# A two-layer graph network: used columns of the adjacency matrix listed on the chip and gathered by indirect DMA

## Chip, cores, metric

One core of a Trainium2 chip (trn2). Times are device microseconds (us) of one execution; each figure is the median of the fast runs of one kernel. Engines: PE is TensorE (PEld its weight loads), DVE VectorE, ACT ScalarE, POOL GpSimd, SP SyncE. "Row tile" means 128 of the 2708 nodes; there are 22, the last with 20 rows.

## The reference, cut

```python
def _gat_head(h, node_adj, edge_adj, W, a):
    hW = h @ W
    hp = (node_adj > 0).astype(hW.dtype) @ hW
    hm = (node_adj < 0).astype(hW.dtype) @ hW
    e_plus = leaky_relu(concatenate([hp, hm], axis=1) @ a, ALPHA)[:, 0]
    # ... e_minus for negative entries
    att = where(edge_adj > 0, e_plus[None, :], NEG_INF)
    att = softmax(where(edge_adj < 0, e_minus[None, :], att), axis=1)
    return att * edge_adj @ hW

# layer 0; adj0 is adj without its diagonal d
h = relu(layernorm(x))
edge = gru(adj0 @ h, h, edge weights)
node = gru(mean over 3 heads of _gat_head(h, adj0, adj0, W_i, a_i), h, node weights)
x = x + d * edge + d * node
# layer 1: the softmax over neighbours has one logit per row, so it is a mean over neighbours
h = relu(layernorm(x))
x = x + layernorm(mean over j with adj[i, j] > 0 of (h @ W)_j) * gamma + beta
```

`x` is 2708 x 256 and `adj` 2708 x 2708 in float32. Of `adj` 10,885 entries off the diagonal are set, 0.15%, all of them positive; the diagonal is at least 0.05.

## The kernel before

It treats `adj` as dense: everywhere 22 chunks of 128 columns for each row tile. The three parts that the change replaces:

```python
# 1. slabs of adj^T (512 columns): node support and logits
for n0, nn in slabs:
    for m0, g in mgroups:
        nc.sync.dma_start(at[:mr, :g, :nn], src...)            # adj^T
        nc.vector.tensor_scalar(pm, at, 0.0, None, op0=ALU.is_gt)
        # ... mm with is_lt, mask written to DRAM for layer 1
        for j in range(g):
            for c in range(KC):
                nc.tensor.matmul(pns[:, c, :nn], lhsT=h_sb[:mr, m, c*P:(c+1)*P], rhs=at[:mr, j, :nn], ...)
            # ... two mask products for the logits
    # ... logits to all partitions (E), edge GRU for each row tile

# 2. attention by rows of adj
for t in range(NT):
    nc.sync.dma_start(A[:r], adj[t*P : t*P + r, :])
    for i in range(HEADS):
        nc.gpsimd.memset(L[:r], NEG_INF)
        nc.vector.copy_predicated(L[:r], pos[:r], E[:r, i, :])
        nc.vector.copy_predicated(L[:r], neg[:r], E[:r, HEADS + i, :])
        nc.vector.tensor_reduce(nmax[:r], L[:r], AX.X, ALU.max, negate=True)
        nc.scalar.activation(L[:r], L[:r], AF.Exp, bias=nmax[:r], accum_out=den[:r])
        nc.gpsimd.tensor_tensor(L[:r], L[:r], A[:r], op=ALU.mult)
        # 22 transposes of L, 22 copies from PSUM, 22 products with h
    # ... head weights, node GRU

# 3. layer 1: 22 x 22 blocks of the mask times h in three bf16 parts
for t in range(NT):
    for m in range(NT):
        for s, (c0, cn) in enumerate(parts):
            nc.tensor.matmul(ps[:r, :cn], lhsT=mask[:, m, t*P : t*P + r], rhs=hs[:, m, c0:c0+cn], ...)
```

## Time and profile before

| | before |
|---|---|
| median of 4 runs | 2337.9 us (2334.8 to 2341.2) |
| PE / DVE / POOL busy | 1999 / 1411 / 632 us |
| layer norm and head vectors | 0 to 84 us |
| slabs, edge GRU | 84 to 640 us (556) |
| dense attention, node GRU | 640 to 2062 us (1422) |
| layer 1: preparation, mask products | 2062 to 2342 us (77 + 203) |

An engine is "busy" while it runs instructions; where PE is near 100% of a stage, as in the slabs, PE bounds it, and where no engine is, as in attention, they take turns. The lines are in the prediction.

### The profile page before, as it was taken

What the parts mean: (1) busy time and instruction counts of PE and PEld (TensorE: products, weight loads), DVE (VectorE), ACT (ScalarE), POOL (GpSimd) and SP (SyncE); (2) the same over time, 40 slices, a digit from 0 to 9 for tenths busy, and PEclk for the clock granted to TensorE, in tenths of its full rate; (3) what the DMA queues carried; (4) which work ended last, traced back from release to release, by engine and by line L of the source; (5) the groups of instructions that cost most, each with busy time, mean ns of one, the idle gap of its engine ahead of it and who ended that gap; (6) DMA issues with size and microseconds to landing.
All of it is one profiled execution on the core that took longest, in us unless ns stands there. A gap on an engine that the chain in (4) does not pass through costs nothing.

```text
span 2341.6 us, 21972 instructions
## 1 busy us (share of the span) xinstructions
PE 1998.8 (85%) x8718; PEld 1298.2 (55%) x8718; DVE 1410.9 (60%) x1655; ACT 568.2 (24%) x1100; POOL 631.6 (27%) x270
## 2 busy tenths in 40 slices
PE   3899999999938888898888888888888898869985
PEld 2333334343526666676666666666666676436774
DVE  5422233322285868878687778686868878355444
ACT  1110101000112333333333333333333333222000
POOL 1000000000034443344333443334443343201323
PEclk9979798987968999998999999999999999978998
DMA  3322130301110000000000000000000000030000
GB/s 102 129 81 68 51 91 31 117 21 33 56 40 24 25 24 24 24 24 24 24 24 24 24 18 17 14 24 24 24 24 24 25 4 1 1 136 6 15 17 14
DMA packets 52591, 86.40 MB, mean 37 GB/s; under 512 B 8536, under 2 KB 32378, under 8 KB 49782
## 3 DMA queue, kind: packets, MB, share of 16 engines
q1 hardware_dynamic: 26782, 70.35, 8.9%
q10 hardware_dynamic: 25708, 14.66, 2.1%
q8 instruction: 68, 1.11, 0.2%
q14 instruction: 33, 0.27, 0.0%
HBM read 74.89 MB, written 10.11 MB: 36 GB/s over the span
## 4 chain that ended last, share of the span: by engine, by line
PE 54%; DVE 24%; issue 9%; POOL 6%; ACT 4%; DMA 2%; ACTq 0%; POOLq 0%; SPq 0%; DVEq 0%
PE pq L355 17%; DVE L L333 11%; PE pns L276 10%; DVE L L334 5%; DVE nmax L336 5%; PE pn L166 4%; PE prz L161 3%; PE prz L159 3%; PE ptr L349 3%; PE pn L167 2%; PE pb L298 2%; ACT wT L353 2%; PE prz L162 2%; POOL L L332 2%; PE pe L284 2%
## 5 line engine op out<-in xcount | busy, mean ns | idle before, releaser
L355 PE MATMUL pq<-h_sb,wT 128*128 128x256 f32 (+2 forms) x2904 | 753.0, 405 | 198.6 <-ACT wT L353 193.8
L355 PEld LDWEIGHTS pq<-h_sb,wT 128*128 128x128 f32 (+2 forms) x2904 | 537.9, 196 | 335.8 <-ACT wT L353 244.3
L341 POOL TENSOR_TENSOR L<-L,A 128x2708 f32<-128x2708 f32 (+1 forms) x66 | 393.3, 5960 | 489.5 <-ACT L L338 489.5
L333 DVE COPY_PREDICATED L<-pos,E 128x2708 f32<-128x2708 uint8 (+1 forms) x66 | 394.3, 5976 | 131.1 <-POOL L L332 130.9
L332 POOL MEMSET L<- 128x2708 f32 (+1 forms) x66 | 155.3, 2354 | 898.2 <-DVE x_sb L182 580.7
L353 ACT COPY wT<-ptr 128x512 f32<-128x512 f32 (+3 forms) x462 | 204.6, 479 | 465.9 <-PE ptr L349 465.6
L349 PE MATMUL ptr<-ident,L 128*128 128x128 f32 (+2 forms) x1452 | 223.6, 287 | 32.2 <-POOL L L341 32.2
L276 PE MATMUL pns<-at,h_sb 128*128 128x512 f32 (+2 forms) x528 | 239.7, 574 | 1.1 <-DVE at L263 1.1
L338 ACT ACTIVATE L<-L,nmax 128x2708 f32<-128x2708 f32 (+1 forms) x66 | 168.6, 2555 | 240.4 <-DVE nmax L336 240.4
L349 PEld LDWEIGHTS ptr<-ident,L 128*128 128x128 f32 (+2 forms) x1452 | 176.2, 146 | 85.3 <-POOL L L341 33.3
L334 DVE COPY_PREDICATED L<-neg,E 128x2708 f32<-128x2708 uint8 (+1 forms) x66 | 218.3, 3310 | 1.8
L336 DVE TENSOR_REDUCE nmax<-L 128x1 f32<-128x2708 f32 (+1 forms) x66 | 196.0, 2971 | 1.5
L440 PE MATMUL ps<-hs,mask 128*128 128x256 bf16 (+4 forms) x1452 | 164.3, 272 | 18.0 <-ACT hp L445 18.0
L440 PEld LDWEIGHTS <-mask 128*128 128x128 fp8e4 (+3 forms) x1452 | 137.7, 96 | 44.5 <-issue 27.0
L175 DVE TENSOR_TENSOR o<-h_sb,n 128x256 f32<-128x256 f32 (+1 forms) x44 | 134.2, 3050 | 14.0 <-ACT n L173 11.1
L276 PEld LDWEIGHTS pns<-at,h_sb 128*128 128x128 f32 (+1 forms) x528 | 87.2, 192 | 99.4 <-issue 95.4
L253 DVE TENSOR_SCALAR pm<-at 128x1536 fp8e4<-128x1536 f32 (+3 forms) x48 | 39.1, 815 | 159.4 <-PE pe L284 152.5
L171 DVE SCALAR_TENSOR_TENSOR n<-rz,pn 128x256 f32<-128x256 f32 (+1 forms) x44 | 18.3, 416 | 189.9 <-PE pn L167 184.8
L113 POOL TENSOR_TENSOR rstd<-v,mhalf 128x1 f32<-128x1 f32 x66 | 36.2, 551 | 304.3 <-DVE v L111 262.0
L340 DVE RECIPROCAL rden<-den 128x1 f32<-128x1 f32 (+1 forms) x66 | 10.8, 163 | 134.6 <-ACT L L338 134.6
L366 PE MATMUL pes<-qT,w 128*128 128x128 f32 (+1 forms) x528 | 84.7, 295 | 0.3 <-ACT qT L133 0.3
L366 PEld LDWEIGHTS pes<-qT,w 128*128 128x128 f32 x528 | 78.1, 214 | 3.0 <-issue 0.4
(133 smaller groups left out, 1730.2 us busy)
## 6 DMA issues: line engine op xcount, KB each, us to landing
A<-in_adj_dram SPq DMA_DIRECT2D x21, 1354.0 KB, 5.7
at<-in_adjT_dram SPq DMA_DIRECT2D x35, 768.0 KB, 4.3
mask<-mask_dram SPq DMA_DIRECT2D x21, 338.5 KB, 6.2
mask_dram<-pm ACTq DMA_DIRECT2D x35, 192.0 KB, 4.6
x_sb<-in_x_dram SPq DMA_DIRECT2D x1, 2688.0 KB, 10.8
out_dram<-y ACTq DMA_DIRECT2D x21, 128.0 KB, 1.7
at<-in_adjT_dram SPq DMA_DIRECT2D x7, 222.0 KB
w<-in_L_gnn_gat_W_dram SPq DMA_DIRECT2D x3, 256.0 KB, 2.8
```

What stands on the lines that cost most here:

```text
L276: nc.tensor.matmul(pns[:, c, :nn], lhsT=h_sb[:mr, m, c * P : (c + 1) * P], rhs=at[:mr, j, :nn], start=first, stop=last,)
L332: nc.gpsimd.memset(L[:r], NEG_INF)
L333: nc.vector.copy_predicated(L[:r], pos[:r], E[:r, i, :])
L334: nc.vector.copy_predicated(L[:r], neg[:r], E[:r, HEADS + i, :])
L336: nc.vector.tensor_reduce(nmax[:r], L[:r], AX.X, ALU.max, negate=True)
L338: nc.scalar.activation(L[:r], L[:r], AF.Exp, bias=nmax[:r], accum_out=den[:r])
L341: nc.gpsimd.tensor_tensor(L[:r], L[:r], A[:r], op=ALU.mult)
L349: nc.tensor.transpose(ptr[:mr, j, :r], L[:r, (m + j) * P : (m + j) * P + mr], ident[:r, :r])
L353: nc.scalar.copy(wT[:mr, :g, :r], ptr[:mr, :g, :r])
L355: nc.tensor.matmul(pq[:r], lhsT=wT[:mr, j, :r], rhs=h_sb[:mr, m + j, :], start=(m + j == 0), stop=(m + j == NT - 1),)
L366: nc.tensor.matmul(pes[:, c, :r], lhsT=w[:, k, i, c * P : (c + 1) * P], rhs=qTs[i][:, k, :r], start=(i == 0 and k == 0), stop=(i == HEADS ...
L440: nc.tensor.matmul(ps[:r, :cn], lhsT=mask[: rows(m), m, t * P : t * P + r], rhs=hs[: rows(m), m, c0 : c0 + cn], start=(m == 0 and s == 0), ...
```

## The change

Its intent: do work only for columns that are used. Columns are cut into five ranges (`NG` = 5). For each row tile and range the kernel lists the used columns, at most 128 of them, with compares and small products; an indirect DMA then gathers these rows of adj^T (`S`), and all products run on 5 gathered chunks instead of 22. The tables that the products need (h with the exponentials of the logits; later h of layer 1 in three bf16 parts) are written to DRAM and gathered with the same lists. Flags (among them more than 128 used columns, negative entries, large logits, a row without any entry) decide whether the old program runs after all. The GRUs now work on slabs of four row tiles. Cut to its core:

```diff
+    bad = compressed_path(tc, *args)
+    with tc.If(bad > 0):
+        general_path(tc, *args)          # the old program

+            for j in range(NT):                                   # lists
+                nc.sync.dma_start(at[:mr], adjT[j*P : j*P + mr, :])
+                nc.vector.tensor_reduce(reach[:mr, j, :NFULL], at..., AX.X, ALU.max, apply_absolute_value=True)
+                nc.vector.tensor_scalar(used[:, j, :], reach[:, j, :], 0.0, None, op0=ALU.is_gt)
+                # place = rank of each used column in its range, by two small products
+                for t in range(NT):
+                    nc.vector.tensor_scalar(onehot[:, t, :], iota1, place[:, j, t:t+1], None, op0=ALU.is_equal)
+                # ... for each range g: 22 products onehot x (tile, row, 1, logit parts) add up lists[g]
+                # when range g is complete:
+                    for t in range(NT):
+                        nc.gpsimd.indirect_dma_start(
+                            S[:, t, g, : rows(t)], None, adjT,
+                            bass.IndirectOffsetOnAxis(ap=idxa[:, g, t:t+1], axis=0), element_offset=t*P)
+                        if edges[g] < t*P + rows(t) and edges[g+1] > t*P:      # own block: drop the diagonal
+                            nc.vector.tensor_scalar_add(own, ia[:, t:t+1], -float(t*P))
+                            nc.vector.scalar_tensor_tensor(blk, iota0, own, blk, op0=ALU.not_equal, op1=ALU.mult)
+            # ... masks, logits, exp, the columns of htab

+            for s in range(...):                                  # main: slabs of 4 row tiles
+                for t in ts:
+                    for g in range(NG):
+                        nc.gpsimd.indirect_dma_start(hg, None, htab, ...idxh[:, g, t:t+1]...)
+                        nc.scalar.copy(sv[:, 0, :r], S[:, t, g, :r])
+                        for i in range(HEADS):
+                            nc.vector.tensor_scalar(sv[:, 1+i, :r], S[:, t, g, :r], hg[:, D+i:D+i+1], None, op0=ALU.mult)
+                        for k in range(KC):
+                            nc.tensor.matmul(pq[k][:, :, :r], lhsT=hg[:, k*P:(k+1)*P], rhs=sv[:, :, :r], ...)
+                    # ... counts, normalizers (dg, pb, rb), nsT and qT
+                ds, ns = gru(edge, nsT, ...); ...; ds, ns = gru(node, esT, ...)
+                    # in gru: nc.gpsimd.tensor_tensor(d, h, n, op=ALU.subtract)
+                    # after it: nc.gpsimd.tensor_tensor(osum, osum, n, op=ALU.add)
+                # ... transposes pt, x of layer 1, its layer norm (rs by POOL's power), rows of h1tab

+        for t in range(NT):                                       # layer 1
+            for g in range(NG):
+                nc.gpsimd.indirect_dma_start(hg, None, h1tab, ...idxh[:, g, t:t+1]...)
+                for s, (c0, cn) in enumerate(parts):
+                    nc.tensor.matmul(ps[:r, :cn], lhsT=mask[:, t, g, :r], rhs=hg[:, c0:c0+cn], ...)
+            # ... mean, product with W, layer norm (rs by POOL's power), out
```

## The prediction

> **What bounds the kernel now.** I read first the shares and the forty slices, then the busy time by stage (I set the stage borders at the first and last instruction of each program part), then the groups and single rows.
>
> ```profile
> PE 1998.8 (85%) x8718; PEld 1298.2 (55%) x8718; DVE 1410.9 (60%) x1655; ACT 568.2 (24%) x1100; POOL 631.6 (27%) x270
> PE   3899999999938888898888888888888898869985
> ...
> DVE  5422233322285868878687778686868878355444
> ```
>
> PE is busiest, but only in slices 3 to 11 does it stand at 9. By stage (columns: length, then busy time and instructions of PE, weight loads, DVE, ACT, POOL; granted clock; DMA share; GB/s):
>
> ```profile
> 84.00:640.00 556.00, 553.17 (x1353) 208.69 (x1352) 164.92 (x303) 52.38 (x102) 0.00 (x0) 0.89 0.23 71
> 640.00:2062.00 1422.00, 1190.14 (x5565) 890.18 (x5564) 1061.22 (x483) 460.95 (x817) 549.19 (x136) 0.92 0.06 21
> ...
> 2139.00:2342.00 203.00, 164.63 (x1455) 137.81 (x1453) 92.90 (x437) 13.18 (x45) 59.75 (x88) 0.96 0.04 15
> ```
>
> The slabs of adj^T (556 us) are bound by TensorE alone. The dense attention (1422 us, 61% of the span) has PE at 84% and DVE at 75%, neither full: PE, DVE and POOL take turns. The mask products of layer 1 (203 us) are PE again. All three multiply by matrices whose entries are nearly all zero. What attention costs:
>
> ```profile
> L355 PE MATMUL pq<-h_sb,wT 128*128 128x256 f32 (+2 forms) x2904 | 753.0, 405 | 198.6 <-ACT wT L353 193.8
> ...
> L341 POOL TENSOR_TENSOR L<-L,A 128x2708 f32<-128x2708 f32 (+1 forms) x66 | 393.3, 5960 | 489.5 <-ACT L L338 489.5
> L333 DVE COPY_PREDICATED L<-pos,E 128x2708 f32<-128x2708 uint8 (+1 forms) x66 | 394.3, 5976 | 131.1 <-POOL L L332 130.9
> ...
> L336 DVE TENSOR_REDUCE nmax<-L 128x1 f32<-128x2708 f32 (+1 forms) x66 | 196.0, 2971 | 1.5
> ```
>
> **What the Trainium skill says.**
> 1. "TensorE: Matmul & The Clock Gate", Back-to-back issue gap: N columns take N/2.4 + 2.5 ns warm. The trace agrees, if a float32 product counts as four passes (two instructions of two): the rows below start 1.71 us apart for two products of 512 columns, 0.855 us each. That stretch has clock 1.00; the slab stage as a whole got 0.89.
>
> ```profile
> 283.30 1.88 PE L159 MATMUL prz<-whh_e,hT 128*128 128x512 f32 x4
> 285.01 1.88 PE L161 MATMUL prz<-wih_e,nsT 128*128 128x512 f32 x4
> ```
>
> 2. "VectorE: DVE Perf Modes", The perf-mode tier table: tensor_reduce has only 1x, tensor_scalar 2x in float32 and 4x in bf16. It agrees for float32: the reduce above takes 2.97 us over 2708 columns, the compare of line 325 over the same columns 1.56 us.
> 3. "SBUF — State Buffer", Who interferes with whom: a DVE instruction with two SBUF inputs and a GpSimd instruction that reads SBUF block each other, and so do a DVE two-port mode and the descriptor writing of a DMA issued from GpSimd. The first half shows here: the same copy takes 3.20 us alone and 8.90 us when it starts just behind POOL's product. The second has no instance before.
>
> ```profile
> 965.10 3.20 DVE L333 COPY_PREDICATED L<-pos,E 128x2708 f32<-128x2708 uint8 x1
> ...
> 977.95 5.91 POOL L341 TENSOR_TENSOR L<-L,A 128x2708 f32<-128x2708 f32 x1
> 978.02 8.90 DVE L333 COPY_PREDICATED L<-pos,E 128x2708 f32<-128x2708 uint8 x1 [0.43 <-POOL L L332]
> ```
>
> 4. "DMA: Bandwidth & Descriptors", Latency and other measured facts, gives a DMA issued from GpSimd about 1 us to the first byte ("the Q7 emission overhead"), and Anatomy of one DMA a fixed 2.0 us. The kernel before issues none, so its trace has no price for the new main operation. I take P = 1.3 us of POOL per gather of 128 rows and 2.5 to 3 us to landing: an estimate from that page, the largest unknown here.
>
> **Is the fallback taken?** I counted the inputs that the reference makes: over 22 row tiles and 5 column ranges the used columns number 91 on average and 126 at most, against 128 places; no entry is negative, the diagonal is at least 0.05, the logits stay under 13.1 against a limit of 40. The branch should skip the old program, at the price of a register load and a jump, some 7 us at the end (a guess).
>
> **The change part by part.** Removed: everything above, but for the GRUs and the layer norm. Now three stages, each waiting for the one before through a table in DRAM, so their times add.
>
> *Lists.* adj^T is read once, 22 loads of 1354 KB; such a load lands in 5.7 us (section 6, A), 125 us in all, beneath DVE. DVE per tile: absolute-max reduce 2.97 + 0.15 for the remainder; diagonal 0.28; used, place, running sum about 0.55; 22 one-hot compares of 128 bf16. One compare I put at 0.17 us: 4x mode, and line 461 (0.23 us, a pointer scalar) against 0.16 for its like without. Sum 3.1 + 0.28 + 0.55 + 22 x 0.17 = 7.7 us, x22 = 169. Layer norm 22 x 0.87 (bn_stats 0.41, aggregate 0.17, two of 0.15) = 19; constants 6; own blocks 26 x 0.4 = 10. DVE total 204 us; with some 13% of waits (place waits on PE, own blocks on gathers) 230. Of the 110 gathers 88 lie beneath; the last 22 cannot start before the last list: 22 x 1.3 + 3 = 31 us. Masks, logits, exp, the table write and the first gather: 15 us. Together **276 us**.
>
> *Main, six slabs.* PE, warm: per tile 10 products of 512 columns x 0.855 = 8.5 us, x21 = 180, the 20-row tile 2; counts 110 x 0.1 = 11; row normalizers 21 x 0.64 (384 columns) = 13; the GRUs and head weights 60 products a slab x 0.855 = 51.3, x5 = 256, and 15 for the 148-column slab; transposes 6. Sum 483 us. At clock 0.88, as in the slab stage, 548; 8% of waits, 590; the last slab's tail to the table, 12. **602 us**. The others hide beneath: DVE per tile 15 scalings x 0.2 + 2.6 = 5.6 us and some 21 per slab, ACT less, POOL 5 x 1.3 + 2.7 = 9.2 us a tile against 24 of PE. The GRUs cost what they did: before, per four tiles, 4 x (5 x 0.855 + 6 x 0.43) = 27 us each, now 20.5 as the bias products are gone.
>
> *Layer 1.* PE per tile: 18 bf16 products x 0.133 (line 440: 66 in 8.78 us) = 2.4, plus transposes and weights 1.4. DVE 3.4. POOL 5 x 1.3 + 0.55 (line 113) = 7.05, so POOL bounds: x22 = 155, and 20 for the loads at the start and the tail. **175 us**.
>
> Sum 276 + 602 + 175 + 7 = **1060 us**, 0.45 of before.
>
> **Rivals.**
> A. *The gathers bound everything.* 330 x P is 430 us at 1.3. At P = 2.0 (descriptor writing blocked by DVE's two-port compares and scalings, point 3) lists grow by 15 and layer 1 by 77 us: 1150. At P = 1.0: 1020. Against more: the main stage has POOL slack up to P of some 4.
> B. *Waits in order.* If engines ran in program order, POOL's rsqrt of a tile would hold the next tile's gathers, and each layer-1 tile would cost 5P + 7.5 us, +130 us; slab ends would idle PE some 25 us each, +130 us: 1300. Against: in the trace of before the order is not that of the program; bn_stats of tile 2 runs ahead of tile 0's scaling. Such a schedule overlaps tiles, but it was fixed without knowing the true gather time, so some of B may show.
> C. *Fallback taken, or a costly branch.* Taken: 1060 + 2336 = 3400. The count speaks against it; 126 of 128 is tight but whole numbers are exact.
> D. *Compares at 1x* (0.26 us each): lists +44 us, 1105.
>
> **Range and chances.** Middle 1060. Down: P of 1.0 and few waits, 548 for main, give some 960. Up: A at P = 1.6 with D and half of B give 1040 + 160 = 1220. Range **940 to 1220**. Even the worst of A, B and D together stays under 1500, so faster is 0.97; only C is slower, 0.02.
>
> **What would show it.** Right: no instruction of the old attention; one reduce of 2.9 us per adj^T tile; DVE near full until some 230 us with PE low; then some 600 us of PE at 9 and clock near 0.88; then POOL issuing without a break while PE is half idle. Wrong: POOL solid in the main stage, or gaps between gathers in layer 1 that end on the rsqrt (B); one-hot compares above 0.2 us (D); gathers far from 1.3 us; a span above 3000 us.

## The result, and the profile after

The changed kernel takes **1011.3 us** (1009.5 to 1013.8, 4 runs), correct; the ratio to the kernel before is 0.4325 (95% interval 0.4312 to 0.4338). A ratio here is the mean time of one kernel's fast runs over that of the other's of the same rounds, so not quite the ratio of the medians quoted. 1060 us was predicted, 940 to 1220 as range.

From the first page, what answers to the lines of before:

```profile
PE 700.8 (69%) x2722; PEld 370.6 (37%) x2722; DVE 516.9 (51%) x1911; ACT 198.4 (20%) x498; POOL 402.8 (40%) x443
...
PE   0424452332618998899889988998899883665655
...
DVE  3888984495645523742464247324732563343345
...
POOL 1010077755445511440144014401440214777772
```

Three stages can be seen in the slices (25 us each): DVE at 8 to 9 in slices 2 to 6 and mostly at 4 to 6 behind them, with PE low, at first; PE at 8 to 9 in the middle; POOL at 7 with PE at half at the end. I set the borders at the first gather of a row of `htab` (303) and the last write to `h1tab` (842):

```profile
0.00:303.00 303.00, 106.88 (x842) 75.31 (x842) 209.89 (x881) 44.47 (x109) 120.08 (x143) 0.95 0.49 154
303.00:842.00 539.00, 495.15 (x1356) 228.11 (x1356) 241.25 (x809) 135.48 (x345) 164.76 (x168) 0.97 0.18 49
842.00:1012.00 170.00, 98.78 (x524) 67.17 (x524) 65.73 (x222) 18.44 (x44) 117.94 (x132) 0.81 0.63 180
```

(Columns as in the prediction's table by stage: window and length, busy time of PE, weight loads, DVE, ACT, POOL, granted clock, DMA share, GB/s.) Lists took 303 us (predicted 276), main 539 (602), layer 1 with the branch 170 (175 + 7). The main stage is TensorE's, 92% busy; the other two are not.

The new groups (busy us, mean ns of one | idle time before them, and what ended it):

```profile
L932 POOL DMA_INDIRECT hg<-htab,idxh x110 | 111.8, 1016 | 96.0 <-PE pd L950 58.0 <-issue 25.9 <-PE pq L943 4.3
L805 POOL DMA_INDIRECT S<-in_adjT_dram,idxa x110 | 106.2, 965 | 78.1 <-DVE own L811 39.8 <-issue 32.3 <-DVE ih L800 5.6
L1076 POOL DMA_INDIRECT hg<-h1tab,idxh x110 | 105.3, 957 | 37.2 <-issue 29.1 <-PE ps L1080 4.9 <-PE ph L1096 1.4
...
L772 DVE TENSOR_SCALAR onehot<-iota,place 128x128 bf16<-128x128 bf16 x484 | 83.0, 270 | 0.0
...
L813 DVE SCALAR_TENSOR_TENSOR S<-iota,own,S 128x128 f32<-128x128 f32 x24 | 8.4, 351 | 43.4 <-DMA S<-in_adjT_dram,idxa 43.3
```

Two things are to be seen. A gather costs POOL about the same for rows of 512 bytes (S), 1056 (htab) and 1544 (h1tab). And the zeroing of own blocks (the entries on the diagonal), 8 us of work, stood 43 us waiting for gathers, while the gathers stood 40 us waiting for DVE (`<-DVE own`). In VectorE's order of time:

```profile
148.37 4.65 DVE L772 TENSOR_SCALAR onehot<-iota,place 128x128 bf16<-128x128 bf16 x28
164.09 0.35 DVE L813 SCALAR_TENSOR_TENSOR S<-iota,own,S 128x128 f32<-128x128 f32 x1 [11.08 <-DMA S<-in_adjT_dram,idxa]
```

The compares run 28 in 4.65 us, 0.166 us each; then DVE idles 11 us until a gathered block lands, with the next tile's reduce and compares in its queue behind.

At the border of two slabs (times of a row: start, duration):

```profile
394.28 1.27 POOL L911 TENSOR_TENSOR d<-hT,n 128x512 f32<-128x512 f32 x1 [25.06 <-ACT n L909]
395.50 1.27 POOL L996 TENSOR_TENSOR osum<-osum,n 128x512 f32<-128x512 f32 x1
395.58 1.74 DVE L912 SCALAR_TENSOR_TENSOR d<-rz,d 128x512 f32<-128x512 f32 x1 [2.19 <-POOL d L911]
...
398.58 0.33 PE L1006 MATMUL pt<-ident,osum 128*128 128x128 f32 x1 [1.63 <-DVE osum L997]
...
402.51 0.68 DVE L912 SCALAR_TENSOR_TENSOR d<-rz,d 128x512 f32<-128x512 f32 x1
```

The same DVE operation takes 0.68 us alone and 1.74 us when it starts beside POOL's, and the transposes of PE wait for the end of this chain (`osum` is the sum of both GRUs' outputs). In layer 1, POOL (`rs` is the inverse deviation of a layer norm):

```profile
933.20 0.95 POOL L1076 DMA_INDIRECT hg<-h1tab,idxh  x1 [0.30 <-issue]
...
934.46 0.95 POOL L1076 DMA_INDIRECT hg<-h1tab,idxh  x1 [0.31 <-issue]
...
935.71 0.96 POOL L1076 DMA_INDIRECT hg<-h1tab,idxh  x1 [0.30 <-issue]
...
936.97 0.95 POOL L1076 DMA_INDIRECT hg<-h1tab,idxh  x1 [0.30 <-PE ps L1080]
...
937.95 0.57 POOL L612 TENSOR_TENSOR rs<-v,mhalf 128x1 f32<-128x1 f32 x1
```

A gather starts every 1.26 us (0.95 busy, 0.30 of "issue") and runs without a stop; five of them and one `rs` make the 6.8 us in which a row tile passes.

### The profile page after: what moved, and what is told of

It is laid out like the page before. It is cut to its first block, busy times and chain, and to the rows that moved or that the text cites. A ratio compares the mean times of both kernels' runs of the same rounds, so it can differ in the third digit from the quotient of the medians.

```text
span 1012.0 us, 9694 instructions
## 1 busy us (share of the span) xinstructions
PE 700.8 (69%) x2722; PEld 370.6 (37%) x2722; DVE 516.9 (51%) x1911; ACT 198.4 (20%) x498; POOL 402.8 (40%) x443
## 4 chain that ended last, share of the span: by engine, by line
PE 46%; DVE 21%; POOL 14%; issue 9%; DMA 7%; ACT 2%; ACTq 0%; SPq 0%; POOLq 0%; DVEq 0%
PE gr L888 19%; PE pq L943 14%; POOL S L805 7%; PE gr L989 5%; DVE onehot L772 4%; DVE reach L743 4%; POOL hg L1076 3%; POOL rs L612 2%; DVE sv L939 2%; PE pb L969 2%; DMA hg<-h1tab,idxh 1%; PE ps L1080 1%; DVE d L912 1%; PE ph L1096 1%; DMA b_e<-in_L_gnn_edge_bhh_dram 1%
## 5 line engine op out<-in xcount | busy, mean ns | idle before, releaser
L943 PE MATMUL pq<-sv,hg 128*128 128x512 f32 (+1 forms) x440 | 202.5, 603 | 0.0
L932 POOL DMA_INDIRECT hg<-htab,idxh x110 | 111.8, 1016 | 96.0 <-PE pd L950 58.0
L805 POOL DMA_INDIRECT S<-in_adjT_dram,idxa x110 | 106.2, 965 | 78.1 <-DVE own L811 39.8
L1076 POOL DMA_INDIRECT hg<-h1tab,idxh x110 | 105.3, 957 | 37.2 <-issue 29.1
L939 DVE TENSOR_SCALAR sv<-S,hg 128x128 f32<-128x128 f32 (+1 forms) x330 | 87.3, 322 | 56.6 <-DMA hg<-htab,idxh 21.9
L943 PEld LDWEIGHTS pq<-sv,hg 128*128 128x128 f32 x440 | 83.5, 200 | 85.1 <-issue 77.0
L772 DVE TENSOR_SCALAR onehot<-iota,place 128x128 bf16<-128x128 bf16 x484 | 83.0, 270 | 0.0
L743 DVE TENSOR_REDUCE reach<-at 128x21 f32<-128x2688 f32 (+1 forms) x22 | 64.8, 2947 | 0.0
L888 PE MATMUL gr<-hT,whh_e 128*128 128x512 f32 (+1 forms) x144 | 63.3, 564 | 0.5 <-ACT got L792 0.5
L888 PE MATMUL gr<-nsT,wih_e 128*128 128x512 f32 (+1 forms) x144 | 61.2, 544 | 0.5 <-ACT nh L902 0.5
```

Source lines behind the costliest of these rows:

```text
L743: nc.vector.tensor_reduce(reach[:mr, j, :NFULL], at[:mr, : NFULL * P].rearrange("p (t r) -> p t r", r=P), AX.X, ALU.max, apply_absolute_va ...
L772: nc.vector.tensor_scalar(onehot[:, t, :], iota1, place[:, j, t : t + 1], None, op0=ALU.is_equal)
L805: nc.gpsimd.indirect_dma_start(S[:, t, g, : rows(t)], None, adjT, bass.IndirectOffsetOnAxis(ap=idxa[:, g, t : t + 1], axis=0), element_off ...
L888: nc.tensor.matmul(ps[:, :R], lhsT=w[:, q * P : (q + 1) * P], rhs=src, start=(i == 0), stop=(i == len(terms) - 1))
L932: nc.gpsimd.indirect_dma_start(hg, None, htab, bass.IndirectOffsetOnAxis(ap=idxh[:, g, t : t + 1], axis=0))
L939: nc.vector.tensor_scalar(sv[:, 1 + i, :r], S[:, t, g, :r], hg[:, D + i : D + i + 1], None, op0=ALU.mult)
```

## The experiments

The theory: the gain comes from fewer products; lists are held by DVE and by the hand-over between DVE and POOL, main by TensorE, layer 1 by POOL's price for a gather. All experiments leave the branch out, so the first run is their base. Times of stages are those of the profiled execution.

### e1: without the branch

```diff
-    bad = compressed_path(tc, *args)
-    with tc.If(bad > 0):
-        general_path(tc, *args)
+    compressed_path(tc, *args)
```

> The conditional old program is left out; the rest is the changed kernel (1011.3 us). Theory: the branch costs what I guessed for it, about 7 us, so this kernel takes about 1004 us. Rival: the branch is nearly free because the condition is ready long before the last rows are out, then 1008 to 1011 us. This kernel is also the base for the next experiments. Its result stays correct on these inputs.

Measured: 1007.7 us, ratio 0.4308 (0.4288 to 0.4327). The branch costs 3.6 us by medians, but the intervals of the two ratios overlap, so this is not clear of the noise. The two profiles agree with it: from the issue of the last output to the end it is 5.6 us with the branch and 2.5 without. 7 was guessed. Stages as in the kernel with the branch: first gather of `htab` at 302.4, last write of `h1tab` at 838.1.

### e2: the own blocks after the lists

```diff
-                        if edges[g] < t*P + rows(t) and edges[g+1] > t*P:
-                            ...                                  # zeroing right behind the gather
             for t in range(NT):
+                for g, _, _ in parts_of(t):                      # before the masks
+                    nc.vector.tensor_scalar_add(own, ias[:, g, t:t+1], -float(t*P))
+                    nc.vector.scalar_tensor_tensor(blk, iota0[:, :r], own, blk, op0=ALU.not_equal, op1=ALU.mult)
                 nc.vector.tensor_scalar(mask[:, t, :, :r], ...)
```

> Without the branch, and with the zeroing of each list's own block moved out of the list loop to just before the masks, after all lists. Theory: in the list stage VectorE stands 43 us behind gathers that have just been issued (the zeroing waits for a gathered block, and the next tile's reduce and compares wait behind it), and GpSimd in its turn waits for the next list. Without these waits the stage should end 25 to 40 us earlier, the zeroing's own wait should fall from 43 us to under 10, and the whole takes 30 us or so less than the same kernel without this edit. Rival: the stage is held by GpSimd's gathers (110 at 1.26 us) or by the loads of adj transposed, and the waits only move: then less than 10 us is gained. Result stays correct.

Measured: 985.9 us, 21.8 less than e1 in the same rounds; main begins at 279.5 instead of 302.4. The group, and the longest wait of DVE in this stage now (us in total, times, longest):

```profile
L817 DVE SCALAR_TENSOR_TENSOR S<-iota,own,S 128x128 f32<-128x128 f32 (+1 forms) x25 | 8.4, 346 | 4.0 <-DMA S<-in_adjT_dram,idxa 3.8
```

```profile
DVE mask L820 <- DMA S<-in_adjT_dram,idxa: 34.2, 14, 25.9
```

The gathers of S before (the changed kernel) and now (min/median/max ns, first to last start):

```profile
L805 POOL DMA_INDIRECT S<-in_adjT_dram,idxa x110: 949/955/1169, 128.1 to 290.8; - x110
```

```profile
L804 POOL DMA_INDIRECT S<-in_adjT_dram,idxa x110: 951/955/1136, 128.1 to 267.4; - x110
```

The hand-over was real and cost 23 us, a little under the 25 to 40 expected: 40 us of waiting vanished, and half came back as the wait of the masks for the last gathers. The rival is in part true too: DVE's last compare now ends at 213 us instead of 263, so the last list is ready 50 us earlier, but the 110 gathers, which start at 128.1 as before, now follow each other without a gap (1.28 us from start to start) and are through only at 268. From here on POOL, and not DVE, sets the end of this stage.

### e3: plain loads in the main stage

```diff
-                        nc.gpsimd.indirect_dma_start(hg, None, htab, ...)
+                        nc.sync.dma_start(hg, htab[(4*g + t%4)*P : (4*g + t%4 + 1)*P, :])
```

> Without the branch; the main stage's 110 gathers of rows of htab are replaced by plain loads of 128 rows in a block, issued from SyncE. The result is wrong on purpose; every shape and product stays. Theory: the gathers are hidden in the main stage, which is held by TensorE (500 of 526 us) and by short stops at the borders of slabs: the stage changes by less than 10 us. Rival: the stops at the borders, about 9 us a slab, come from gathers issued too late by GpSimd: then the stage gets 30 to 50 us shorter.

Measured: 990.6 us. Its output is wrong, which doesn't matter for the time. Main went from 535.7 to 519.3 us, 16 less: between the two expectations. PE's waits in the main stage, e1 and then e3:

```profile
PE pt L1004 <- DVE osum L995: 19.3, 12, 2.0
...
PE pb L967 <- DVE dg L962: 11.6, 4, 2.9
```

```profile
PE pt L1002 <- DVE osum L993: 18.9, 12, 1.8
...
PE pb L965 <- DVE dg L960: 0.9, 1, 0.9
```

(`dg` is a diagonal block with the normalizers of a row tile.) So the gathers are not quite hidden: without them in POOL's queue the wait for `dg` is gone. TensorE stands idle 32 us of the stage instead of 43; the rest of the 16 us is its own busy time, 487 instead of 492 us at a granted clock of 0.99 instead of 0.97. The wait for `osum` is untouched and has another cause (e7).

### e4: plain loads in layer 1

```diff
-                nc.gpsimd.indirect_dma_start(hg, None, h1tab, ...)
+                nc.sync.dma_start(hg, h1tab[(4*g + t%4)*P : (4*g + t%4 + 1)*P, :])
```

> Without the branch; layer 1's 110 gathers of rows of 1544 bytes are replaced by plain loads of blocks of 128 rows, issued from SyncE. Same bytes, wrong result on purpose. Theory: layer 1 is held by GpSimd, which spends 5 x 1.26 + 0.55 = 6.85 us on each row tile (the trace shows tiles 6.8 us apart): without the gathers a tile is held by TensorE (about 4.3 us busy) or the transfers (0.99 MB, 4 to 5 us), and the whole falls by 35 to 50 us. Rival: the bytes or the memory hold it (DMA share 0.68): then it falls by under 12 us.

Measured: 962.4 us, 45 less than e1. Its output is wrong, which doesn't matter for the time. From the last write of `h1tab` to the end it is 125 us instead of 167. The same bytes come in 42 us less, so their number did not hold this stage; the gathers' issue did. The plain loads read whole blocks and not scattered rows, so this run alone does not exclude slow scattered reads; POOL without a gap above, and e6, do.

### e5: half of each gather

```diff
-                    hg, None, h1tab, bass.IndirectOffsetOnAxis(ap=idxh[:, g, t:t+1], axis=0)
+                    hg[:64], None, h1tab, bass.IndirectOffsetOnAxis(ap=idxh[:64, g, t:t+1], axis=0)
                 )
+                nc.sync.dma_start(hg[64:], h1tab[(4*g + t%4)*P : (4*g + t%4)*P + 64, :])
```

> Without the branch; each of layer 1's 110 gathers fetches 64 rows instead of 128, and a plain load from SyncE brings 64 others, so bytes and products stay. Result wrong on purpose. It tells whether GpSimd's 0.95 us a gather is a price for each index or for each instruction. If for each index: about 0.5 us of work, 0.8 us apart, 4.5 us a tile, and the whole falls by about 40 us against the kernel without the branch, as with plain loads (45 us). If for each instruction: 0.95 us stays and the time changes by less than 5 us.

Measured: 1020.6 us; ratio 0.4354, 11 us more than e1 by ratios. Its output is wrong, which doesn't matter for the time. POOL in layer 1:

```profile
936.65 0.90 POOL L1074 DMA_INDIRECT hg<-h1tab,idxh  x1 [0.30 <-DMA hg<-h1tab]
937.86 0.91 POOL L1074 DMA_INDIRECT hg<-h1tab,idxh  x1 [0.30 <-PE ph L1095]
```

```profile
L1074 POOL DMA_INDIRECT hg<-h1tab,idxh x110 | 100.4, 913 | 38.5 <-issue 24.0 <-PE ps L1079 4.9 <-DMA hg<-h1tab,idxh 2.5
```

With half the indices a gather takes 0.91 instead of 0.95 us and they start 1.21 us apart instead of 1.26. The price is one for each instruction, nearly whatever it carries. The time itself was expected to stay; it rose, and not in POOL (first to last gather 141 us, in e1 146). The last plain half was issued at 996.2, 10 us behind the last gather: so it seems that the added loads, not the gathers, end this run.

### e6: two bf16 parts in layer 1's table

```diff
-    HB = 3 * D + 4
+    HB = 2 * D + 4
-        parts = [(2 * D, D + 1), (D, D), (0, D)]
+        parts = [(D, D + 1), (0, D)]
```

(and the third part is no longer made)

> Without the branch; layer 1's table holds each number in two bf16 parts instead of three: rows of 1032 bytes instead of 1544, and two products instead of three with each gathered chunk. Theory (layer 1 is held by GpSimd's issue of gathers): tiles stay 6.8 us apart and the whole falls by less than 8 us, though a third of the bytes and of TensorE's work there are gone. Rival (bytes, or TensorE at its lower clock): layer 1 falls by a fifth to a third, 30 to 50 us. The error of the result should grow, but perhaps stay small enough.

Measured: 999.8 us, correct; ratio 0.4265, 10 us under e1 by ratios. From the first to the last gather of layer 1 it is 145.9 us (e1: 146.1), with a third of the bytes and of the products gone. The gain lies in front of layer 1: the last write of `h1tab` is at 826.3 instead of 838.1 (less than 8 us was expected in all), and from the last gather to the end it is 24 us instead of 18. Theory confirmed again, by the same view.

### e7: element-wise work of the main stage on VectorE

```diff
-                    nc.gpsimd.tensor_tensor(d[:, :R], h_[q], n[:, :R], op=ALU.subtract)
+                    nc.vector.tensor_tensor(d[:, :R], h_[q], n[:, :R], op=ALU.subtract)
-                    nc.gpsimd.tensor_tensor(osum[:, q, :R], osum[:, q, :R], ns[q][:, :R], op=ALU.add)
+                    nc.vector.tensor_tensor(osum[:, q, :R], osum[:, q, :R], ns[q][:, :R], op=ALU.add)
```

> Without the branch; the main stage's 20 subtractions and 10 additions of 128x512 move from GpSimd to VectorE. Theory: at the border of two slabs they hold VectorE (its own op of the same shape took 1.74 us beside one and 0.68 us otherwise) and delay GpSimd's gathers; plain loads in place of the gathers gained 16.6 us, so a free GpSimd should gain 8 to 20 us. Rival: VectorE is the later of the two at the borders, and 30 more operations of 0.69 us in its queue cost as much as they save: within 5 us either way.

Measured: 979.2 us, ratio 0.4179, 30 us under e1 by ratios; main 509 instead of 536. More than expected, and in part for another reason than the one I wrote down. PE's waits:

```profile
PE pb L967 <- DVE dg L962: 6.9, 6, 1.5
...
PE pt L1004 <- DVE osum L995: 2.2, 2, 1.7
```

It is the wait for `osum` that went (19.3 to 2.2 us): the chain tanh, subtract, multiply, add, transpose at the end of a slab got shorter. POOL took 1.27 us for a subtraction of 128x512, DVE takes 0.69; and the multiplication behind it fell from 1.00 us on average to 0.69, as nothing runs beside it on POOL. The wait for `dg` fell only to 6.9. TensorE's idle time in the stage falls from 43 to 23 us; the other 6 of the 27 us are its busy time, at a clock of 0.98.

### e8: early normalisation, on top of e2

```diff
-        tc.tile_pool(name="p0x", bufs=4) as p0x, tc.tile_pool(name="p0h", bufs=2) as p0h
+        tc.tile_pool(name="p0h", bufs=4) as p0h
-                h = p0x.tile([P, D], F32, name="h")
+                h = S[:, t, 0:2, :].rearrange("p g r -> p (g r)")
```

> As the run with the zeroing moved (985.9 us), and besides: layer 0's normalised rows have a buffer for every tile (they lie in S before the gathers need it) instead of four, and the one-hot blocks four buffers instead of two. Theory: the normalisation goes in bursts of four tiles between loads of adj transposed and is done at 107 us; list 0 can't be built before, so VectorE's compares stand still. With the rows loaded at once the first list gather leaves well before 100 us instead of at 128 us, and the whole is 12 to 25 us under the run with the zeroing moved. Rival: the first 100 us are held by the 29 MB of loads, and less than 6 us is gained.

Measured: 953.1 us, ratio 0.4065, 34 us under e2 by ratios: more than expected. The gathers of S now start at 93.2 us instead of 128 and end at 237.7 (min/median/max ns, first to last start):

```profile
L804 POOL DMA_INDIRECT S<-in_adjT_dram,idxa x110: 951/956/1136, 93.2 to 237.7; - x110
```

Main begins at 250.0. So the loads of adj^T did not hold the first 100 us. This run changes the row buffers and the one-hot buffers at once, so which of them did is not shown. Nor is DVE much earlier through its lists: its last compare ends at 209 us, in e2 at 213. It is POOL's row of gathers, which set the end in e2, that starts 35 us and ends 30 us earlier here; the last 22 start at 210.8, right behind the last list. The two edits of the list stage give 52 us together, and DVE is now busy 204 of 250 us.

### e9: all together; e10: with two parts

e9 is e8, e7, the sums of the GRU biases moved behind the lists (DVE had stood 8 to 12 us for their loads at the start), and layer 1's `rs` without POOL:

```diff
-            nc.gpsimd.tensor_tensor(rs[:r], v[:r], mhalf[:r], op=ALU.pow)      # layer 1 only
+            nc.scalar.activation(rs[:r], mv[:r, 1:2], AF.Sqrt, bias=epst[:r])
+            nc.vector.reciprocal(rs[:r], rs[:r])
```

> All together, three bf16 parts kept: the zeroing after the lists, early normalisation, the sums of the biases made after the lists, element-wise operations of the main stage on VectorE, and in layer 1 the inverse deviation from ScalarE's square root and VectorE's reciprocal instead of GpSimd's power. Theory: the gains lie in different stages and add up: 953 us less 28.5 (element-wise), less 22 x 0.55 = 12 (GpSimd bounds layer 1 and loses that work), less some 4 (biases): about 908 us. Rival: layer 1 is held by more than GpSimd's instruction time (transfers, TensorE), so the 12 us don't come: about 920 us. If gains overlap: above 925 us.

> As the run with all together, and layer 1's table in two bf16 parts. Theory: layer 1 stays at GpSimd's 5 x 1.26 us a tile, so only the preparation of the table at the ends of slabs gets shorter: 5 to 12 us less than with three parts. If layer 1 with three parts is no longer held by GpSimd, more than 15 us less. The result should be taken as correct, as it was with this edit alone.

Measured: e9 917.4 us (916.2 to 919.6), correct, ratio 0.3921: 9% less than the changed kernel, though without its fallback. The stages are 249, 509 and 156 us. In layer 1:

```profile
L1081 POOL DMA_INDIRECT hg<-h1tab,idxh x110: 942/947/1183, 761.2 to 899.0; - x110
```

138 us for 109 steps is 1.26 us a gather, now without gaps; 146 it was with `rs` on POOL. So 8 of the 12 us came there, and with the tail layer 1 is 11 us shorter than in e8. The list stage gained only 1 us of the 4 from the biases, the main stage 27. The time lies between 908 and the rival's 920, nearer to the latter, but not for the rival's reason, as layer 1's gain did come.

e10 took 926.9 us, 9 more than e9, against both expectations. Layer 1's gathers again span 138 us; behind the last of them it is 2 us longer. The main stage is 8 us longer (517): its products of 512 columns take 615 instead of 600 ns on average and the granted clock is 0.98 in two stretches where e9 has 1.00; PE waits 4.2 instead of 1.3 us for `xt`. The order of PE's instructions differs as well. Which of these is cause is not settled; with e6 faster by 10 us than its base, two parts have no clear worth.

### e11: e3 and e7 together

> Without the branch, with both edits of the main stage: element-wise operations on VectorE (28.5 us gained alone) and plain loads in place of the gathers of htab (17 us gained alone); result wrong on purpose. Theory: they take away different waits of TensorE at the borders of slabs. The element-wise move shortens the chain from the last tanh of a slab to its transposes (TensorE's wait there fell from 20.4 to 3.2 us), the plain loads free GpSimd for the inverse deviations and hence VectorE's later operations (TensorE's wait for dg fell from 11.6 to 1.2 us). Then the gains add up to 40 to 46 us, 962 to 968 us in all. Rival: both cure the same lateness of GpSimd: then about 977 us, as with the element-wise move alone.

Measured: 1035.0 us (1029.2 to 1038.2): slower than its base by 27 us by medians and 25 by ratios, which nothing here expected. Its output is wrong, which doesn't matter for the time. The main stage alone, 331.0 to 834.9, is 504 us: 32 less than e1, where 27 + 16 would be 43. So the two gains overlap in part. (TensorE's idle time falls from 43 to 20 us; e3 alone took 12 of it and e7 21.) But the list stage, which the edits don't touch, took 29 us longer, and layer 1 about 200 instead of 167. In the list stage DVE stood before compares with nothing to wait for that the profile shows (e7 has no such wait):

```profile
DVE onehot L770 <- issue: 28.5, 36, 1.1
```

36 gaps of about 0.45 or 1.1 us between compares that otherwise follow each other at 0.165. PE shows the same kind of gap in layer 1 (20.3 us before `ph`, 18.0 before `pt`). All four runs were as slow, while the kernel before took its usual 2343 us in the same rounds. The cause stays open; the total of this run says nothing about its edit, and only the main stage was used.

## Why the prediction was right, point by point

The time was 4.6% below the middle of the prediction, well inside its range. The sum was 276 + 602 + 175 + 7; measured are 303 + 539 + 170 (with the branch). Two terms were off by more than 20 us, in opposite directions: lists 27 too low, main 63 too high. That they partly cancel is luck; that main and not lists had the larger error is why the time came out below the middle.

- **Where the gain comes from: right.** No instruction of the old attention is left, and PE's busy time falls from 1999 to 701 us.
- **Lists, 276 us: 27 too low; the term that failed is "some 13% of waits".** DVE's work was right: 204 predicted, 194 measured up to the last compare (at 263 us, predicted 230), with compares 0.166 us apart (0.17), so rival D is out. But the waits of DVE up to there, as the profile names them, add up to 67 us instead of 26, and 41 of these are own blocks; so the sign "DVE near full until some 230 us" did not come either. The cause of these 41 is shown by e2. What the prediction did not have is the floor that e2 and e8 uncover: in e2 the 110 gathers take 139 us of POOL without a break, so the moment of the first one counts. The last 22 gathers took 28 us (31), masks to table 11 (15).
- **Main, 602 us: 63 too high; the step that failed is "at clock 0.88, as in the slab stage".** PE's work was right within 3% (483 warm; 495 busy), but the clock granted was 0.97, not 0.88. Waits and the last tail were put at 42 and 12 us; TensorE stood idle 44 us (539 - 495). So of the 63 us, 53 are TensorE's own time (put at 548 with that clock, measured 495) and 10 its waits. These lie where expected, at slab borders, and at the start, where TensorE waits 10.5 us for the first gather (e1); e7 and e3 show what those at the borders were. Why this stage is granted more than the slabs of before, with PE 92% busy instead of 99%, no run here tells; e7 and e9, with PE at 95%, have 0.95 to 1.00 too.
- **Layer 1, 175 us: right, with its cause.** POOL bounds it: e4, e5 and e6 took away the gathers, half of their indices, and a third of the bytes and products, and only the first made the stage shorter. Five gathers and `rs` were put at 7.05 us a tile; 6.8 were measured.
- **P = 1.3 us a gather: right** (1.26), and so rival A (P = 2.0) did not come. The prediction does not say how 1.3 follows from the page's figure of about 1 us, so its closeness is partly luck. The 2.5 to 3 us to landing were near as well: medians of 2.7 (S) and 3.2 us. The Trainium skill's "SBUF — State Buffer", Who interferes with whom, would have VectorE's two-port modes block the descriptor writing. Not much of it shows here: a gather took 0.965 us on average in the lists, beside the bf16 compares, and 0.957 in layer 1. In the main stage it is 1.016, but most of the excess lies in 16 gathers that don't start beside scalings:

```profile
329.78 0.56 DVE L964 TENSOR_TENSOR dg<-ident,den 128x384 f32<-128x384 f32 x1
329.85 1.31 POOL L932 DMA_INDIRECT hg<-htab,idxh  x1 [0.30 <-DVE den L962]
331.47 0.96 POOL L932 DMA_INDIRECT hg<-htab,idxh  x1 [0.30 <-issue]
331.51 0.68 DVE L939 TENSOR_SCALAR sv<-S,hg 128x128 f32<-128x128 f32 x3 [1.17 <-DMA hg<-htab,idxh]
```

A gather beside scalings takes 0.96 us. 16 of the 110 take 1.30 to 1.32, and each of them starts some 0.07 us behind the start of DVE's product for `dg`; whether that is their cause, no run tests. The other half of that section, two inputs on DVE against POOL, does show: 1.74 against 0.68 us.
- **Rival B in part.** Waits in order cost 23 us in the lists (e2) and some 24 at slab borders (TensorE's idle time in the main stage of e11 against e1), not the 260 us of that rival. In layer 1 `rs` did not make POOL stop between tiles; it only added its own 0.57 us.
- **Rival C, the fallback: not taken.** The branch costs some 4 us by medians, not clear of the noise (e1). The fallback itself ran in no run here.
- **Slips in the working.** The slices of PE in which it stands at 9 are not only 3 to 11, but 18, 33, 37 and 38 too. Rival B's layer 1, 5P + 7.5 = 14 us a tile against 7.05, is +153 us and not +130. The upper end of the range, "1040 + 160 = 1220", does not add up: it is 1200, and A at P = 1.6 (+40), D (+44) and half of B (+130) on 1060 give 1274. Nothing hung on it, as the time lies near the middle.

The Trainium skill's "GPSIMD Engine Reference", 4.1 Engine selection, puts two-input element-wise work on GpSimd at about twice VectorE's time. The trace agrees: 1.27 against 0.69 us for 128x512 in float32. I had read the cost of it, but asked only whether POOL was full; the cost lay in the chain that PE waits for.

## What to carry to other kernels

When sparse operands are listed on the chip, count the gathers and not their bytes: each is an instruction of POOL at a fixed price, so fill all 128 rows, and keep other work off that engine in a stage that it bounds. Let the first of them leave early: where all go through one queue, their number times the price is the least time from there to the end. An operation that waits for a gather just issued should not stand in the queue of the engine that prepares the next gather. And an engine that is 30% busy can still hold the bound one, if it does a link of the chain at the end of each round.

## What the Trainium skill lacked or had wrong

- "DMA: Bandwidth & Descriptors", Latency and other measured facts, gives about 1 us to the first byte of a DMA issued from GpSimd, but I found no price for a stream of gathers. Here: 0.95 us of POOL and 0.30 us between two, 1.26 us from start to start, for rows of 512, 1032, 1056 and 1544 bytes alike; 0.91 and 1.21 us with 64 indices instead of 128.
- "SBUF — State Buffer" has one copy as its example of descriptor writing blocked by VectorE, some 620 ns of a DMA that become some 3100, but no figure for gathers among many short instructions. Here: 0.965 us on average among bf16 compares and 0.96 beside float32 scalings, against 0.957 in layer 1; 16 of the main stage's 110 took 1.30 to 1.32 us.
- "TensorE: Matmul & The Clock Gate" ties the clock to how busy TensorE has been, but that did not help to tell which clock a stage gets: 0.89 in the slabs of the kernel before (busy 553 of 556 us), 0.97 in the main stage after (495 of 539), 0.81 in layer 1 (99 of 170). This was the largest error of the prediction.
- No page that I found explains gaps without a releaser like those of e11: 36 of about 0.45 or 1.1 us, 28.5 us in all, in compares that were not changed.
